# Two thirds of x loaded ahead of w1, w1's taps copied to contiguous places, small constants loaded later, and four turn copies moved to VectorE, in a dilated-attention and bottleneck kernel

## The chip, the cores and the metric

One core of one Trainium2 chip. The metric is the device time of one execution in microseconds (us), median of three runs. The work is fp32 throughout. An fp32 matmul runs as two passes over the array, so the profile's instruction counts on TensorE (PE) are twice the kernel's matmuls.

## The reference, cut to what matters

`x` is (4, 256, 64, 64). Layer 0 makes 49 attention weights for every pixel from a 7x7 convolution with dilation 2 and a 1x1 convolution, and then sums the 49 dilated shifts of `x` with them. Layer 1 is a bottleneck with batch norms that take their statistics from the data.

```python
# layer 0: w1 is (128, 256, 7, 7), w2 is (49, 128, 1, 1)
k = conv(x, w1, padding=6, dilation=2) + b1
k = conv(k, w2) + b2                                  # 49 logits a pixel
attn = softmax(k, axis=1)
xp = jnp.pad(x, ((0, 0), (0, 0), (6, 6), (6, 6)))
shifts = stack([xp[:, :, 2*u : 2*u+64, 2*v : 2*v+64] for u in range(7) for v in range(7)], axis=1)
x = einsum('bkchw,bkhw->bchw', shifts, attn)
# layer 1
h = relu(bn(conv(x, w1_1x1)))                         # 256 -> 64 channels
h = relu(bn(conv(h, w2_3x3, pad=1)))                  # 64 -> 64
h = bn(conv(h, w3_1x1))                               # 64 -> 256
out = relu(h + x)
```

## The kernel before, in words

**The convolution.** The two convolutions of layer 0 are one 7x7 convolution from 256 channels to 49, with the kernel w2·w1. Along the rows (the tap index u) the kernel uses a Winograd-like transform with the points ±0.4, ±0.8, ±1.25, ±2.5 (`PAIRS`), 0 and infinity. There are five **passes** over the data, one for each pair of points and one for the last two. In each, VectorE makes transformed rows of x (`xi`) out of sorted rows of x (`slots`) with `scalar_tensor_tensor` steps, all of which have the line L152, and PE multiplies them with the transformed weights `ut`, column tap by column tap (`column_convs`, L263). Columns come in four strips; `acc[i][s]` is the PSUM bank of strip s and of point i of the pair. [...]a first half of channels (up to about 293 us) runs all five passes, and each pass's sums are put aside in DRAM (`put_aside`, L287 and L288). The second half takes them back (`put_back`, L607, and ScalarE's copy from `bks` into PSUM, L608), adds its own and writes the logits (`outputs`: ScalarE's copy of one bank, L591, then VectorE's sum and difference, L592 and L593, and four steps of L152).

**The start of the first half.** x comes in three pieces of 16, 24 and 24 rows (`PIECES`), each with a load for each of four images: 12 loads in all, 0.62 or 0.93 MB each, on SP's DMA queue, into four rotating `raw` buffers. `sort_x` reads a piece and writes its rows to `slots` by four copies: rows by their remainder of 4, with the columns ahead of the rows, so that every element that a copy reads is apart from the next. Three of the four copies run on ScalarE (L171) and the last on POOL. `early(n, strips, parts)` makes those transformed rows of pass 0 that piece n completes, on VectorE; `even` and `odd` are three steps each and `mix` two.

The transformed weights need w1: half of it is two loads of 1.6 MB each (`load_w1`), into one buffer `w1raw`, so the second half's load waits until the first half's last reader is done. `product(w1raw, half, v, bank)` makes the weights of column tap v: seven matmuls (one for each u, L326), whose stationary operand is `w1raw[:, :, u * K7 + v]`, 128 elements that lie 49 elements apart; the moving operand `powers` are the w2 taps times the powers of the points. ScalarE evicts the result in two copies (L337, L338), and VectorE makes difference and sum of them (L342, L343). There are seven products for each half of the channels. The first `column_convs` need all seven products and the sums of pass 0.

**Around 293 us** the first half's passes end, `column_convs` of the second half's pass 0 start, and small constants are loaded on ScalarE's queue: the identity `ident`, `w1m`, `pavg`, `pdiff`, `w3m` and (L502 to L504) ten loads of batch-norm parameters into `bn12` and `bn3`. The tiles `bn12` and `bn3` are in the pool `keep`, which is open from the kernel's start; the other constants are in the pool `late`, which opens at L488 in memory that the first half's buffers leave.

In pass 2, every visit of a strip or of two strips has an `apply_factor` ahead of it, a VectorE step over two groups of 17 rows (17 = NR - 2; "17-wide" in the text).

**The end of layer 0.** For each of four strips VectorE and ScalarE make the softmax (`exponents`: VectorE's maximum and difference, ScalarE's exponential; `shares`: VectorE's sums and products, into padded rows `pads`). `turn(s, h)` transposes half a strip on PE (eight transposes, L567, in each of four steps j) into two of the eight PSUM banks, used in turn. Two copies for each step (g = 0 and 1) put the result into `amat` in `arena`. They are ScalarE's (L574), but with `shared=True` the g = 1 copies are VectorE's (L572). From 503 us on, PE sums the shifts with these weights (`gather`, L746), and conv1, conv2 and conv3 follow with their batch norms.

**What sets the order.** The engines' instruction orders are partly written by hand: within `manual_schedule(engines=...)` the named engines run in the order of the program. From the start to the end of layer 0's first half this holds for VectorE and PE, and for ScalarE and SP too in the block of L366 to L392. Where an engine isn't named, a scheduler places its instructions. Each engine runs its queue in order: an instruction that waits holds all behind it. The turns' order around the change is

```python
turn(1, 0); exponents(3); shares(2); turn(1, 1); turn(2, 0); shares(3)
load_xt(xtiles[1], *units[0], 1)
turn(2, 1, True); turn(3, 0, True); turn(3, 1, True)
```

Of the kernel before, what the change touches and what calls it, by code (L numbers as in the profile page):

```python
# [48 lines left out]
P = 128  # L49
B, C, H, W = 4, 256, 64, 64  # L50
NH = C // P
K7 = 7
# [41 lines left out]
def conv_seq_kernel(ctx: ExitStack, tc: tile.TileContext, xp, xt, w1, b1, w2t, b2, m1t, g1, be1,  # L94
# [6 lines left out]


    keep = pool(ctx, "keep", 1)
    bn12 = keep.tile([P, 4], F32, name="bn12")
    bn3 = keep.tile([P, 2, NH], F32, name="bn3")
    st1 = keep.tile([P, 2 * NT, 6], F32, name="st1")


# [49 lines left out]

    zero_rows(slots)

    def sort_x(raw, b, r0, n, dst, w0, last=None):

        d = dst.rearrange("p k (w b e) i -> p k w b e i", b=B, e=Q)
        nw = d.shape[2]
        for k in range(2):
            m = r0 // 2 + (r0 // 2 + 3 + k) % 2
            count = ((r0 + n) // 2 - m + 1) // 2
            i = (m + 3) // 2
            for a in range(2):
                lo = 2 * m + a - r0  # L170
                (last if last and k + a == 2 else nc.scalar.copy)(  # L171
                    d[:, k, :, PLACE[b], 2 * a : 2 * a + 2, i : i + count],
                    raw[:, lo : lo + 4 * count - 3 : 4, PAD + 2 * w0 : PAD + 2 * w0 + 2 * nw].rearrange(
                        "p r (w c) -> p w c r", c=2
                    ),
                )
# [60 lines left out]
    def strip(s, n=1):  # L237
        return slice(SW * s, SW * (s + n))
# [37 lines left out]
    with ExitStack() as s1:  # L276
# [13 lines left out]
        with ExitStack() as s2:  # L290
            w1p = pool(s2, "w1p", 1)
            rawp = pool(s2, "rawp", 4)
            b1row = w1p.tile([P, P], F32, name="b1row")
            b2sb = w1p.tile([1, K], F32, name="b2sb")
            ones = w1p.tile([1, P], F32, name="ones")
            nc.scalar.dma_start(out=w2sb, in_=w2t)
            nc.scalar.dma_start(out=b1sb, in_=b1[:, None])
            nc.scalar.dma_start(out=b2sb, in_=b2[None, :])
            nc.gpsimd.memset(ones, 1.0)


            powers = w1p.tile([P, K7, (1 + NP) * K], F32, name="powers")
            points = w1p.tile([P, NP], F32, name="points")
            for i, p in enumerate(PAIRS):
                nc.gpsimd.memset(points[:, i : i + 1], p)
            pv = powers.rearrange("p u (i k) -> p u i k", k=K)
            nc.vector.tensor_copy(pv[:, 0], w2sb.unsqueeze(1).to_broadcast([P, 1 + NP, K]))
            for u in range(1, K7):
                prev = pv[:, 0, 1:] if u == 1 else pv[:, u - 1, :NP]
                nc.vector.tensor_tensor(pv[:, u, :NP], prev, points.unsqueeze(2).to_broadcast([P, NP, K]), ALU.mult)  # L310
            nc.vector.tensor_copy(pv[:, K7 - 1, NP], w2sb)

            def load_w1(half):
                t = w1p.tile([P, P, K], F32, tag="w1", name="w1raw")
                for q in range(2):
                    c0 = half * P + 64 * q
                    nc.sync.dma_start(out=t[:, 64 * q : 64 * q + 64, :], in_=w1[:, c0 : c0 + 64, :])
                return t

            def product(w1raw, half, v, pw):  # L320

                for u in range(K7):

                    o = 0 if u == 0 else (2 + NP) * K if u % 2 else K
                    n = (1 + NP) * K if u in (0, K7 - 1) else NP * K
                    nc.tensor.matmul(  # L326
                        pw[:, o : o + n],
                        w1raw[:, :, u * K7 + v],
                        powers[:, u, :n],
                        start=(u == 0),  # L330
                        stop=(u == K7 - 1),
                        skip_group_check=True,
                    )
                c = slice((6 - v) * K, (7 - v) * K)
                ue = ut[:, half, 1 : 1 + NP, c]
                uo = pw[:, (2 + NP) * K : (2 + 2 * NP) * K].rearrange("p (i k) -> p i k", k=K)
                nc.scalar.copy(ue, pw[:, K : (1 + NP) * K].rearrange("p (i k) -> p i k", k=K))  # L337
                nc.scalar.copy(  # L338
                    ut[:, half, :: 1 + 2 * NP, c],
                    pw[:, : 2 * (1 + NP) * K].rearrange("p (a k) -> p a k", a=2)[:, :, :K],  # L340
                )
                nc.vector.tensor_tensor(ut[:, half, 1 + NP : 1 + 2 * NP, c], ue, uo, ALU.subtract)  # L342
                nc.vector.tensor_tensor(ue, ue, uo, ALU.add)  # L343

            def piece(n, b):
                r0, k = PIECES[n]
                raw = rawp.tile([P, 24, WP], F32, tag="raw", name="raw")
                nc.sync.dma_start(out=raw[:, :k], in_=xp[b, :P, r0 : r0 + k, :])
                sort_x(raw, b, r0, k, slots, 0, nc.gpsimd.tensor_copy)

            def early(n, cols=slice(None), parts=(even, odd, mix)):

                p, _, left = passes[0]
                t0, t1 = READY[n]
                x0, x1 = (xi[:, i, cols, t0:t1] for i in range(2))
                row = rows_of(slots, cols, READY[n])
                if even in parts:
                    even(p, left, row, x0)
                if odd in parts:
                    odd(p, left, row, x1)  # L360
                if mix in parts:
                    mix(p, x0, x1)

            bank = [acc[i][s] for s in range(NS) for i in range(2)]
            spare = [acc[i][s] for s in (NS - 1, 0) for i in range(2)]
            with tc.manual_schedule(engines={mybir.EngineType.Activation, mybir.EngineType.SP}):  # L366
                for b in range(B):
                    piece(0, b)
                w1a = load_w1(0)
                early(0)  # L370
                nc.scalar.copy(b1row, b1sb.to_broadcast([P, P]))
                nc.tensor.matmul(bank[7][:, :K], b1row, w2sb, start=True, stop=False)
                nc.tensor.matmul(bank[7][:, :K], ones, b2sb, start=False, stop=True)
                nc.scalar.copy(bias, bank[7][:, :K])
                for b in range(2):
                    piece(1, b)
                    product(w1a, 0, b, bank[b])
                for b in range(2, B):
                    piece(1, b)
                early(1, strip(0, 2), (even,))  # L380
                for v in range(2, 5):
                    if v > 2:
                        piece(2, v - 3)
                    product(w1a, 0, v, bank[v])
                early(1, strip(0, 2), (odd, mix))
                piece(2, 2)
                product(w1a, 0, 5, bank[5])
                piece(2, 3)
                early(2, strip(0), (even, odd))
                product(w1a, 0, 6, bank[6])  # L390
                early(2, strip(0), (mix,))
                w1b = load_w1(1)  # L392
            early(2, strip(1))
            early(1, strip(2, 2))
            for s in range(2, NS):
                early(2, strip(s))
            u = weights(0, 0)
            column_convs(0, u, True)
            column_convs(1, u, True)
            put_aside(0, 1)  # L400
            product(w1b, 1, 0, spare[0])
            apply_factor(slots, squares[0], NR - 1, strip(0, 2))
            for v in range(1, 5):
                product(w1b, 1, v, spare[v % 4])
            apply_factor(slots, squares[0], NR - 1, strip(2, 2), (0,))
            for v in range(5, K7):
                product(w1b, 1, v, spare[v % 4])
            apply_factor(slots, squares[0], NR - 1, strip(2, 2), (1,))
# [82 lines left out]
    w3m = late.tile([P, C], F32, name="w3m")  # L491
    pavg_sb = late.tile([P, P], F32, name="pavg_sb")
    pdiff_sb = late.tile([P, P], F32, name="pdiff_sb")
    nc.scalar.dma_start(out=ident, in_=z)
    nc.scalar.dma_start(out=w1m, in_=m1t)
    nc.scalar.dma_start(out=pavg_sb, in_=pavg)
# [59 lines left out]
    def turn(s, h, shared=False):  # L556

        row = pads[(2 * s + h) % 3]
        for j in range(4):
# [8 lines left out]
            for g in range(2):  # L568
                dst = amat[:, g, 2 * (2 * s + h) + j % 2, j // 2].rearrange("p (k n) e -> p k n e", k=2)
                src = pt[:, :, 64 * g : 64 * g + 64].rearrange("p (k w) n -> p k n w", k=2)  # L570
                if shared and g:
                    nc.vector.tensor_copy(dst, src)  # L572
                else:
                    nc.scalar.copy(dst, src)  # L574
# [556 lines left out]
```

## Time and profile before

| | us |
|---|---|
| Three runs | 813.88, 808.98, 813.5 (median 813.5) |
| The profiled execution | 815.58 |
| its span on the engines | 813.4 |

Busy time of three engines by stage in the profiled execution, in us:

| Stage, us from the span's start | PE | VectorE | ScalarE |
|---|---|---|---|
| 0 to 20: x pieces sorted, first `early` | 1.3 | 8.8 | 8.2 |
| 20 to 44.6: seven products | 23.5 | 11.3 | 17.8 |
| 44.6 to 56: rest of pass 0's sums | 0 | 11.0 | 4.3 |
| 56 to 100: column convolutions, second half's products | 42.6 | 41.9 | 4.4 |
| 100 to 122 | 19.0 | 19.5 | 13.7 |
| 122 to 309: passes of the first half | 186.6 | 161.1 | 52.7 |
| 309 to 463: passes of the second half | 148.0 | 146.1 | 22.8 |
| 463 to 505: softmax and turns | 40.1 | 28.6 | 30.6 |
| 505 to 813: gather, bottleneck | 280.8 | 145.5 | 146.1 |

The page's slices of the span show the same: a slice is 20.3 us, a digit is the busy share in tenths.

```profile
## 2 busy tenths in 40 slices
PE   0949989999999999979999999999999979979993
...
DVE  4489989999466999999999866122232337764695
ACT  4640165102541102111111268333444436344497
```

PE is at nine tenths nearly everywhere; the first three slices (to 61 us) are the widest hole, and the third (41 to 61 us) is at four tenths. ScalarE and VectorE reach four to six tenths in these three slices, and neither of them is full as an average over 20 us: whether one of them is what PE waits for is read from single waits.

The loads of that stage, from the page's DMA issues (size of each and median time from issue to landing):

```profile
raw<-in_xp_dram SPq DMA_DIRECT2D x36, 608.0 KB, 5.5
```

### The profile page before, as it was taken

Reading aid. Unit: us, or ns where it says so; the run is one execution under the profiler, and the core shown is the slowest. Engines: PE = TensorE matmul, PEld = TensorE weight load, DVE = VectorE, ACT = ScalarE, POOL = GpSimd, SP = SyncE. Lnnn points to the kernel's source line nnn. Section 1 sums busy time; section 2 is a strip of 40 time slices with the busy share of each in tenths; the row PEclk is TensorE's granted clock in tenths of the full one; section 3 lists DMA queues with packets and bytes.
Section 4 is the critical chain, followed back from the end, with each engine's and each line's share of the span. In section 5 each row is a group of like instructions: output and inputs, shape, how many; then the busy total and the mean of one; then the engine's idle time right before and its main releaser. Section 6 shows DMA issues by size and latency. Waiting matters only on the chain. (4 is left out here: it accounts for less than half of the span.)

```text
span 813.4 us, 10844 instructions
## 1 busy us (share of the span) xinstructions
PE 741.9 (91%) x4192; PEld 604.4 (74%) x4192; DVE 573.7 (71%) x673; ACT 300.4 (37%) x587; POOL 79.3 (10%) x137
## 2 busy tenths in 40 slices
PE   0949989999999999979999999999999979979993
PEld 0938968888888888858888889887888864439641
DVE  4489989999466999999999866122232337764695
ACT  4640165102541102111111268333444436344497
POOL 3210000001000010000003002222322200000000
PEclk9979998999999999998999999999999999998997
DMA  8931099703798876111110013666766669360298
GB/s 287 363 158 40 3 330 317 328 36 157 256 331 332 326 292 236 49 40 31 49 40 1 3 56 100 207 207 207 230 225 207 207 220 350 129 205 3 104 373 350
DMA packets 58949, 150.26 MB, mean 185 GB/s; under 512 B 7314, under 2 KB 35602, under 8 KB 54546
## 3 DMA queue, kind: packets, MB, share of 16 engines
q1 hardware_dynamic: 48624, 124.34, 43.4%
q10 hardware_dynamic: 10274, 25.23, 8.0%
q8 instruction: 33, 0.54, 0.3%
q14 instruction: 18, 0.15, 0.1%
HBM read 93.81 MB, written 55.74 MB: 184 GB/s over the span
## 5 line engine op out<-in xcount | busy, mean ns | idle before, releaser
L263 PE MATMUL acc<-arena 128*128 128x343 f32 (+3 forms) x2000 | 383.9, 355 | 20.8 <-DVE arena L152 20.6
L263 PEld LDWEIGHTS acc<-arena 128*128 128x128 f32 x2000 | 323.8, 193 | 79.9 <-issue 14.1
L152 DVE SCALAR_TENSOR_TENSOR arena<-arena 128x1024 f32<-128x1024 f32 (+7 forms) x192 | 290.6, 1560 | 28.0 <-PE acc L263 17.3
L746 PEld LDWEIGHTS acc<-arena,outer 128*128 128x128 f32 x1152 | 129.5, 192 | 8.5 <-issue 6.5
L746 PE MATMUL acc<-arena,outer 128*128 128x128 f32 (+1 forms) x1152 | 130.8, 275 | 1.8 <-POOL outer L126 1.8
L788 DVE BATCH_NORM_STATS2 st<-acc 128x6 f32<-128x512 f32 x16 | 11.1, 695 | 73.8 <-PE acc L780 73.7
L287 ACT COPY sv<-acc 128x392 f32<-128x392 f32 x40 | 19.0, 484 | 103.9 <-PE acc L263 101.7
L171 ACT COPY stage<-raw 128x128 f32<-128x128 f32 x128 | 43.7, 417 | 21.9 <-DMA raw<-in_xp_dram 21.5
L326 PE MATMUL acc<-powers,w1raw 128*128 128x196 f32 (+1 forms) x196 | 45.7, 397 | 6.3 <-DMA w1raw<-in_w_dram 4.9
L326 PEld LDWEIGHTS acc<-powers,w1raw 128*128 128x128 f32 x196 | 44.8, 315 | 6.9 <-issue 6.7
L591 ACT COPY outer<-acc 128x784 f32<-128x784 f32 x8 | 6.5, 812 | 101.1 <-PE acc L263 81.2
L124 ACT COPY outer<-outer 64x2304 f32<-64x2304 f32 x15 | 31.7, 2110 | 32.2 <-DMA outer<-in_xt_dram 27.7
L1007 PE MATMUL pconv<-arena,w3m 64*128 64x512 f32 x128 | 41.2, 635 | 0.0
L152 DVE SCALAR_TENSOR_TENSOR outer<-outer 128x784 f32<-128x784 f32 (+2 forms) x47 | 36.9, 839 | 3.6 <-DMA arena<-y_dram 3.6
L768 DVE COPY bks<-acc 128x256 f32<-128x256 f32 x32 | 12.1, 420 | 35.6 <-PE acc L746 35.6
L1007 PEld LDWEIGHTS pconv<-arena,w3m 64*128 64x128 f32 x128 | 19.1, 185 | 20.5 <-DVE arena L1065 15.4
L1069 ACT ACTIVATE outer<-arena 128x512 f32<-128x512 f32 x50 | 32.8, 749 | 3.7 <-DVE arena L844 1.4
L608 ACT COPY acc<-bks 128x392 f32<-128x392 f32 x40 | 18.5, 488 | 42.5 <-DVE outer L593 33.6
L1065 DVE SCALAR_TENSOR_TENSOR arena<-pconv,arena 128x512 f32<-128x512 f32 x50 | 33.3, 744 | 0.0
L125 POOL COPY outer<-outer 64x2048 f32<-64x2048 f32 x15 | 28.3, 1885 | 44.4 <-DMA outer<-in_xt_dram 43.6
L574 ACT COPY arena<-acc 128x512 f32<-128x512 f32 x52 | 27.1, 715 | 14.8 <-PE acc L567 14.4
L959 PE MATMUL pconv<-outer,arena 128*128 128x512 f32 x72 | 31.1, 592 | 0.0
(144 smaller groups left out, 627.4 us busy)
## 6 DMA issues: line engine op xcount, KB each, us to landing
raw<-in_xp_dram SPq DMA_DIRECT2D x36, 608.0 KB, 5.5
out_dram<-outer ACTq DMA_DIRECT2D x16, 1024.0 KB, 4.1
outer<-in_xt_dram SPq DMA_DIRECT2D x17, 896.0 KB, 5.8
arena<-y_dram SPq DMA_DIRECT2D x25, 512.0 KB, 8.6
fsort_dram<-stage SPq DMA_DIRECT2D x2, 4864.0 KB, 15.1
arena<-fsort_dram SPq DMA_DIRECT2D x8, 1216.0 KB, 10.6
y_dram<-outer SPq DMA_DIRECT2D x16, 512.0 KB, 4.7
aside_dram<-sv ACTq DMA_DIRECT2D x40, 196.0 KB, 5.8
```

Source lines behind the costliest of these rows:

```text
L124: nc.scalar.copy(t[:MID], x[MID:])
L125: nc.gpsimd.tensor_copy(t[MID:, :NT], x[:MID, 1:])
L152: nc.vector.scalar_tensor_tensor(out, in0, scalar, in1, ALU.mult, ALU.add)
L171: (last if last and k + a == 2 else nc.scalar.copy)(d[:, k, :, PLACE[b], 2 * a : 2 * a + 2, i : i + count], raw[:, lo : lo + 4 * count - 3 ...
L263: nc.tensor.matmul(acc[i][d][:, o : o + (hi - lo) * K], xi[:, i, CW * w : CW * w + CW, :].rearrange("p x t -> p (x t)"), u[i][:, lo * K : ...
L326: nc.tensor.matmul(pw[:, o : o + n], w1raw[:, :, u * K7 + v], powers[:, u, :n], start=(u == 0), stop=(u == K7 - 1), skip_group_check=True,)
L574: nc.scalar.copy(dst, src)
L746: nc.tensor.matmul(pt[:, o : o + hi - lo], x[:, i, half * P : (half + 1) * P], a[:, :, blocks, :].rearrange("p x m e -> p m x e"), start=( ...
L959: nc.tensor.matmul(m[k], wu[:, k, j, :], vs[k][:, g, j : j + R, :], start=(j == 0), stop=(j == 1))
L1007: nc.tensor.matmul(pt, w3m[part, half * P : (half + 1) * P], h2[part, slot, q, 512 * i : 512 * (i + 1)], start=True, stop=True)
L1065: nc.vector.scalar_tensor_tensor(v, conv3(b, q, i, half), sc3[:, half : half + 1], v, ALU.mult, ALU.add)
L1069: nc.scalar.activation(dst, v.rearrange("p (r w) -> p r w", w=R), AF.Relu, bias=sh3[:, half : half + 1])
```

## The change

The text of the change moves five things.

**1. Order of loads.** Pieces 0 and 1 of all four images are loaded and sorted ahead of `w1`. Piece 2 is loaded behind it. `bn12` and `bn3` leave the pool `keep` for `late`, so that the ten loads of L502 to L504 can't start before that pool opens.

```diff
     keep = pool(ctx, "keep", 1)
-    bn12 = keep.tile([P, 4], F32, name="bn12")
-    bn3 = keep.tile([P, 2, NH], F32, name="bn3")
...
     pdiff_sb = late.tile([P, P], F32, name="pdiff_sb")
+    bn12 = late.tile([P, 4], F32, name="bn12")
+    bn3 = late.tile([P, 2, NH], F32, name="bn3")
```

**2. Taps.** For the first half of the channels, ScalarE copies the seven taps u of one v (128 partitions x 896 elements) to a contiguous place in a free part of `arena`, three places in rotation; the matmuls read that. The second half's products still read `w1raw`.

```diff
+            def taps(w1raw, v):
+
+                o = UT + (2 + 2 * NP) * KV + K7 * P * (v % 3)
+                t = arena[:, o : o + K7 * P].rearrange("p (u c) -> p u c", c=P)
+                nc.scalar.copy(t, w1raw[:, :, v::K7].rearrange("p c u -> p u c"))
+                return t
+
+            wvs = {}
+
             def product(w1raw, half, v, pw):
 
+                wv = w1raw[:, :, v::K7].rearrange("p c u -> p u c") if half else wvs.pop(v)
                 for u in range(K7):
...
-                        w1raw[:, :, u * K7 + v],
+                        wv[:, u, :],
```

**3. Sorts.** Of piece 1, one copy in four (k + a == 0) goes to VectorE: four copies of 384 elements. Piece 2 is sorted in two halves of columns (192 elements a copy), the first for strips 0 and 1, and the second for strips 2 and 3, outside the block in which ScalarE's order is by hand.

```diff
-            def piece(n, b):
+            def load_piece(n, b):
                 r0, k = PIECES[n]
                 raw = rawp.tile([P, 24, WP], F32, tag="raw", name="raw")
                 nc.sync.dma_start(out=raw[:, :k], in_=xp[b, :P, r0 : r0 + k, :])
-                sort_x(raw, b, r0, k, slots, 0, nc.gpsimd.tensor_copy)
+                return raw
+
+            def sort_piece(raw, n, b, cols=0, strips=NS):
+                r0, k = PIECES[n]
+                on_dve = nc.vector.tensor_copy if n == 1 else None
+                sort_x(raw, b, r0, k, slots[:, :, strip(cols, strips)], WS * cols, nc.gpsimd.tensor_copy, on_dve)
```

**4. The order of the start,** which also sets VectorE's order of `early` sums among the products:

```diff
                 for b in range(B):
-                    piece(0, b)
+                    sort_piece(load_piece(0, b), 0, b)
+                early(0)
+                for b in range(B):
+                    sort_piece(load_piece(1, b), 1, b)
                 w1a = load_w1(0)
-                early(0)
...
-                for b in range(2):
-                    piece(1, b)
-                    product(w1a, 0, b, bank[b])
-                for b in range(2, B):
-                    piece(1, b)
-                early(1, strip(0, 2), (even,))
-                for v in range(2, 5):
-                    if v > 2:
-                        piece(2, v - 3)
+                early(1, strip(0, 2))
+                raws = []
+                wvs[0] = taps(w1a, 0)
+                for v in range(K7):
+                    if v + 1 < K7:
+                        wvs[v + 1] = taps(w1a, v + 1)
                     product(w1a, 0, v, bank[v])
-                early(1, strip(0, 2), (odd, mix))
-                piece(2, 2)
-                product(w1a, 0, 5, bank[5])
-                piece(2, 3)
-                early(2, strip(0), (even, odd))
-                product(w1a, 0, 6, bank[6])
-                early(2, strip(0), (mix,))
+                    if v < B:
+                        raws.append(load_piece(2, v))
+                        sort_piece(raws[v], 2, v, 0, 2)
+                    if v == 0:
+                        early(1, strip(2, 2), (even,))
+                    if v == 4:
+                        early(2, strip(0), (even, odd))
+                    if v == 5:
+                        early(2, strip(0), (mix,))
                 w1b = load_w1(1)
             early(2, strip(1))
-            early(1, strip(2, 2))
+            early(1, strip(2, 2), (odd, mix))
+            for b in range(B):
+                sort_piece(raws[b], 2, b, 2, 2)
             for s in range(2, NS):
                 early(2, strip(s))
```

**5. Turns.** In turn(1,1) and turn(2,0), the g = 1 copies of the odd steps j, four in all, go from ScalarE to VectorE. Both turns stand ahead of `shares(3)` in VectorE's order.

```diff
-                if shared and g:
+                if g and (shared or (j % 2 and (s, h) in ((1, 1), (2, 0)))):
                     nc.vector.tensor_copy(dst, src)
```

The orders of the engines that aren't by hand move with it: around 293 us, VectorE has three `visit` steps and one step of `apply_factor` ahead of the first L592 that stood behind it before, and one 17-wide step less after the fourth output group.

More of the change, by code (lines that the diff above doesn't have):

```diff
@@ L159, in conv_seq_kernel, with sort_x @@
     zero_rows(slots)
-    def sort_x(raw, b, r0, n, dst, w0, last=None):
+    def sort_x(raw, b, r0, n, dst, w0, last=None, first=None):
         d = dst.rearrange("p k (w b e) i -> p k w b e i", b=B, e=Q)
@@ L170, in sort_x @@
                 lo = 2 * m + a - r0
-                (last if last and k + a == 2 else nc.scalar.copy)(
+                (last if last and k + a == 2 else first if first and k + a == 0 else nc.scalar.copy)(
                     d[:, k, :, PLACE[b], 2 * a : 2 * a + 2, i : i + count],
```

## The prediction

> **What bounds the kernel now.** I read the page first: TensorE (PE) is busy 91% of the span, so the question is which PE gaps the change touches. The list of PE's waits, whole run (total us, times, longest), then three stretches of the timeline (start, us, engine, line, operation; in brackets the idle time before it and what ended it). "x98" counts two passes per fp32 matmul, so 49 matmuls.
>
> ```profile
> PE acc L263 <- DVE arena L152: 20.6, 3, 11.5
> ...
> PE acc L567 <- ACT arena L574: 1.8, 2, 1.4
> ```
> The start:
> ```profile
> 0.73 7.15 SPq L348 DMA_DIRECT2D raw<-in_xp_dram  x4
> ...
> 21.03 23.54 PE L326 MATMUL acc<-powers,w1raw 128*128 128x245 f32 x98 [4.95 <-DMA w1raw<-in_w_dram]
> ...
> 56.08 19.13 PE L263 MATMUL acc<-arena 128*128 128x196 f32 x86 [11.51 <-DVE arena L152]
> ```
> PE waits for w1 until 21.0, multiplies the seven products back to back until 44.6, then idles 11.5 us for VectorE's `early` sums. Around 300 us, where the small constants are loaded:
> ```profile
> 292.88 0.34 ACTq L494 DMA_DIRECT2D ident<-in_z_dram  x1
> ...
> 296.00 0.81 ACT L591 COPY outer<-acc 128x784 f32<-128x784 f32 x1 [19.87 <-DVE arena L152]
> ...
> 308.22 0.99 ACT L608 COPY acc<-bks 128x392 f32<-128x392 f32 x2 [5.92 <-DMA bks<-aside_dram]
> ...
> 308.76 36.65 PE L263 MATMUL acc<-arena 128*128 128x49 f32 x204 [0.24 <-ACT acc L608]
> ```
> PE is held 0.24 us by ScalarE's put-back copies: they are just in time, with no slack. The turns:
> ```profile
> 495.51 3.19 DVE L572 COPY arena<-acc 128x512 f32<-128x512 f32 x5 [2.90 <-ACT arena L574]
> 496.26 7.21 PE L567 MATMUL acc<-ident,outer 128*128 128x128 f32 x64
> ```
> VectorE had 2.9 us to spare there; PE did not.
>
> Two prices, by shape (busy, mean ns):
> ```profile
> L171 ACT COPY arena<-raw 128x384 f32<-128x384 f32 x24 | 19.1, 867 | 12.1 <-DMA raw<-in_xp_dram 7.0 <-DVE arena L152 5.1
> ...
> L171 ACT COPY arena<-raw 128x256 f32<-128x256 f32 x12 | 6.5, 630 | 0.1
> ```
> Back to back they step 0.79 and 0.58 us, so a half-column sort of 192 elements steps about 0.46.
>
> [...]sorts,[...] cost (867-630)/128 = 1.85 ns an element; the contiguous 2304-element copy at L124 takes 2110 ns, 0.92 an element. [...]granted clock 0.50 from 122.2 to 128.0, after a 3.1 us gap. [...]here 402 to 419 GB/s between 21 and 36 us.
>
> **Part 1, the start.** Removed: eight small issues of ScalarE's queue before its sorts, with the waits for `bn` and `b1` landings that held SP's first loads to 7.15 us. Moved: four loads of piece 1 (0.93 MB each) go ahead of w1 on SP's queue. Up to w1's landing 2.49+3.74+3.21 = 9.44 MB must pass: 23.0 us at 0.41 MB/us from about 2.9 us, plus 0.8 for the bubble before piece 1 (its buffers wait for the sorts, first freed near 8 us) and 0.8 to the landing: 27.5 instead of 21.0. VectorE in exchange gets `early(1)` of strips 0 and 1 done by about 35 (`early(0)` 12.7 to 22.1, its four new sort copies at 0.85, POOL's price, to 25.5, then 9.7 us); it cost nothing on the path if cheaper.
>
> From 27.5 on ScalarE sets the pace, in this built order: seven `taps` copies of 896 elements, seven evictions (L337+L338, 0.6), and 20 half-column sorts before the fifth eviction, eight of them of the *second* half, which the scheduler slid in between. A `taps` copy (T) is not in the trace: [...] I take 1.35. The first product starts cold, 5.05 as before (21.03 to 26.1), and its eviction waits for it in ScalarE's queue, with all sorts behind. So: 27.5 + 1.35 + 5.05 + 5*0.6 + 20*0.46 + 4*1.35 = 51.5 for the fifth eviction. PE's contiguous weight loads (315 to 193 ns) save about 0.4 us a product, beside that work: nothing. Behind the fifth eviction VectorE has, in order, its pair of L342/L343 (0.72), six `early(2, strip 0)` at 0.74, a pair, two `mix`, a pair: 8.1. Column convolutions start at 59.6, not 56.1: **+3.5**. VectorE is then 3.9 us (three even sums) ahead of its old plan, so PE's 1.36 us wait for L343 at 92.4 goes. Net **+2.2** (T = 0.93: 0.0; T = 1.85: +4.7; w1 a microsecond either way: one). What is late next is unchanged: the 3.1 us gap at 119 hangs on PE's last product through ScalarE's L338 and shifts with it. w1b's load now waits for the seventh `taps` (about 53) and lands by 64, before its use at 80: covered.
>
> **Part 2, small loads later.** The ten `bn` loads now stand on ScalarE's queue among those of 292.9 to 296.0, ahead of the copy at L591. DMA semaphores are used in turn, so a later issue waits for an earlier landing; in the changed program the fourth `bn` issue waits for `w1m`, which landed 8.6 us after its issue at 293.3, at 301.9. Eight issues of 0.55 follow: L591 starts at 306.3, not 296.0. VectorE, which in the new order does three `visit` steps and one `apply_factor` (5.8 us) ahead of L592, comes at 304.6, waits until 307.1 and ends L593 at 310.2. SP's put-back load waits for one of these `bn` landings too: issue near 305, landing 308 to 311.6 (4 to 6.3 us; before 6.3). The last put-back copy ends near 311.2, and PE has nine matmuls (0.384 each) behind that gate where it had six behind 308.8: 314.7 against 311.1, +3.6 (from +1 to +5). At 365 VectorE has one 17-wide step (2.35 us) less before the sums PE waits for: -2.35. Net **+1.25** (-1.4 to +2.7).
>
> **Part 3, four turn copies to VectorE.** They take 4*0.5 us off ScalarE, whose exponentials to 487.1, not these copies, set PE's 1.35 us wait at 488.2: no gain. On VectorE they stand ahead of `shares(3)`, and the last waits for PE's transposes of turn(2,0), 492.2, and ScalarE's copy after them: it ends at 493.65. `shares(3)` (2*2.45 us, begun at 486.45 before) ends at 498.5, and turn(2,1)'s VectorE copies, whose banks PE needs for turn(3,0), start then, not at 495.5. PE's 496.26 becomes 499.2: **+2.9** (0 if the copies overtook, +4 with the `xt` load that waits for `shares(3)`, SP's, 490.7 to 497.6).
>
> **Sum.** 2.2+1.25+2.9 = +6.3. Against the profiled execution's 815.6 (813.4 span and 2.2 around it) that is 821.9; it stands 2.1 above the median 813.5, so I say 820. `bn12`/`bn3` in another pool and the late sorts' 4 ScalarE and 4 POOL pieces (VectorE has 4.8 us of other steps before it needs them) cost nothing; without that cover 2 us.
>
> **Rivals.**
> 1. *Products at PE's pace.* If `taps` and sorts hide, products step 2.7 us (14 loads of 193 ns): 27.5+0.93+5.05+4*2.7+0.6 = 44.9, plus 8.1 = 53.0. Net of the 1.36: -4.4. With the 17-wide step off the path (-2.35) and turns at no cost: -6.8, so 807. For it: contiguous reads, an idle VectorE. Against it: ScalarE's 17.6 us list has no hole.
> 2. *ScalarE's queue becomes the bound* (slower). T at the sorts' rate (+4.7), part 2 at its upper end (+2.7), turns +2.9: +10.3, so 824. It passes 1% from T = 1.6 on with part 2 at its upper end (3.4+2.7+2.9 = 9.0). For it: the measured sort rate and the 8.6 us landing.
> 3. *It doesn't do what it says*: the moved pieces only trade waits, 812 to 816.
>
> **Chances.** Forecast 45%, rival 1 20%, rival 2 30%, rival 3 5%. Within 1% (8.1 us) is about what a measurement of this kernel can tell from no change. Forecast's cases beyond +8.1 (a third) and nearly all of rival 2 give slower 0.40; over half of rival 1, with the clock gap at 122 perhaps closing too (half clock for 5.8 us costs 2.9), gives faster 0.13; the rest 0.47. Range 806 to 828: rival 1's end less a microsecond, rival 2's with turns at +4 and w1 late by one and a half.
>
> **What would show it.** w1 landing near 27.5; a `taps` mean between 0.93 and 1.85 us; products with holes between them and first L263 near 59.6; L591 near 306 plus the shift; PE's first wait for L608 grown from 0.24 to some microseconds; turn(3,0) three microseconds later against turn(2,1). It is wrong if L263 starts before 56, or the small loads land within 3 us.

## The result, and the profile after

| | Before | Changed |
|---|---|---|
| Median of four runs, us | 813.07 | 820.64 |
| Lowest to highest | 808.98 to 813.88 | 818.87 to 821.26 |
| The profiled execution (its span) | 815.58 (813.4) | 820.12 (818.3) |

The ratio is 1.011 [1.0075, 1.0145]: the change made the kernel slower by about 1.1% (by the medians 7.6 us, 0.9%). In the changed kernel's line numbers, L334 is the product's matmul, L322 the `taps` copy, L345 and L346 ScalarE's evictions, L350 and L351 VectorE's, L150 VectorE's sums, L169 the sorts, L261 the column convolutions, L520 to L522 the `bn` loads, L609 and L626 what were L591 and L608, L585 the turns' transposes, L590 and L592 their copies.

PE's waits in the changed kernel (us in total, times, longest). In the kernel before, PE waited 4.9 us for w1's landing, 20.6 for VectorE's sums in three waits of L263, and 0.2 for L608:

```profile
PE acc L334 <- ACT arena L322: 10.0, 5, 4.5
...
PE acc L261 <- DVE arena L150: 3.8, 1, 3.8
...
PE acc L261 <- DVE arena L351: 3.5, 1, 3.5
PE acc L585 <- DVE arena L590: 3.4, 1, 3.4
PE acc L261 <- ACT sv L285: 3.0, 1, 3.0
PE acc L261 <- ACT acc L626: 2.7, 2, 2.3
```

VectorE's sums of pass 0 no longer hold PE as they did: the 11.5 us wait is gone. (In the third slice of the page before, 41 to 61 us, VectorE stands at eight tenths, not at four to six.) What came in its place is 10.0 us that end with a `taps` copy, 3.5 us behind the last product, and two waits: 2.7 for the put-back copies (0.2 before) and 3.4 for VectorE's turn copies (none before). Of the 10.0 us, 2.6 pass before w1 has landed (PE is idle from 26.6, w1 is there at 29.2), so some 7.4 are the copies' own. The starts of the same PE instructions in the two profiled executions show where it adds up:

| PE instruction | Before, us | Changed, us | Difference |
|---|---|---|---|
| First column convolutions | 56.08 | 61.54 | +5.46 |
| Second half's products | 76.77 | 80.36 | +3.59 |
| Column convolutions after them | 100.14 | 102.50 | +2.36 |
| After the gap near 122 | 122.15 | 124.42 | +2.27 |
| After the gap near 365 | 365.25 | 368.26 | +3.01 |
| turn(2,0) | 492.10 | 495.21 | +3.11 |
| turn(3,0) | 496.26 | 502.30 | +6.04 |
| Gathers | 503.30 | 511.00 | +7.70 |
| conv1 after the POOL wait near 563 | 565.28 | 570.83 | +5.55 |
| End of the span | 813.4 | 818.3 | +4.9 |

The start, from the timeline of the changed kernel (start, us, engine, line, operation, idle time before and its releaser):

```profile
29.21 3.49 ACT L322 COPY arena<-w1raw 128x896 f32<-128x896 f32 x2 [2.35 <-DMA w1raw<-in_w_dram]
31.07 7.57 PE L334 MATMUL acc<-powers,arena 128*128 128x245 f32 x28 [4.45 <-ACT arena L322]
...
47.86 2.76 PE L334 MATMUL acc<-powers,arena 128*128 128x245 f32 x14 [1.80 <-ACT arena L322]
48.51 0.36 ACT L345 COPY arena<-acc 128x196 f32<-128x196 f32 x1
48.72 0.56 ACT L169 COPY arena<-raw 128x192 f32<-128x192 f32 x1
49.14 0.28 ACT L346 COPY arena<-acc 128x98 f32<-128x98 f32 x1
49.27 1.42 ACT L169 COPY arena<-raw 128x192 f32<-128x192 f32 x3
...
50.54 1.83 ACT L322 COPY arena<-w1raw 128x896 f32<-128x896 f32 x1
...
53.26 0.30 ACT L346 COPY arena<-acc 128x98 f32<-128x98 f32 x1
...
61.54 13.78 PE L261 MATMUL acc<-arena 128*128 128x196 f32 x71 [3.49 <-DVE arena L351]
```

ScalarE runs without a hole from eviction to sort to sort to `taps`, and PE multiplies for 2.76 us and then waits 1.80 for the next copy. The fifth eviction ends at 53.6, and VectorE's list behind it takes the 8 us to 61.5.

Around 300 us:

```profile
295.44 0.62 ACTq L520 DMA_DIRECT2D bn<-in_be_dram  x1
...
298.15 0.47 ACTq L520 DMA_DIRECT2D bn<-in_g_dram  x1
...
303.92 0.48 ACTq L522 DMA_DIRECT2D bn<-in_be_dram  x1
304.44 0.81 ACT L609 COPY outer<-acc 128x784 f32<-128x784 f32 x1 [27.81 <-DMA bn<-in_be_dram]
304.55 0.99 SPq L625 DMA_DIRECT2D bks<-aside_dram  x2
305.28 0.49 ACT L626 COPY acc<-bks 128x392 f32<-128x392 f32 x1
...
305.83 6.59 PE L261 MATMUL acc<-arena 128*128 128x196 f32 x24 [2.34 <-ACT acc L626]
...
312.74 5.62 PE L261 MATMUL acc<-arena 128*128 128x49 f32 x29 [0.32 <-ACT acc L626]
```

ScalarE's queue stands still from 296.1 to 298.15, ahead of the third of the ten `bn` issues. The issues end at 304.4, and only then do L609 and the put-back copy for which PE waits get their turn. The turns:

```profile
496.19 0.69 DVE L590 COPY arena<-acc 128x512 f32<-128x512 f32 x1 [0.78 <-ACT arena L592]
496.80 0.96 DVE L553 TENSOR_REDUCE sm<-outer 128x16 f32<-128x784 f32 x1
...
501.56 3.18 DVE L590 COPY arena<-acc 128x512 f32<-128x512 f32 x5
...
502.30 8.87 PE L585 MATMUL acc<-ident,outer 128*128 128x128 f32 x64 [3.43 <-DVE arena L590]
```

The fourth moved copy ends at 496.9, `shares(3)` runs from there to 501.6, and the VectorE copies that free PE's banks come behind it. The 64 transposes then take 8.87 us; before they took 7.21.

### The profile page after: what moved, and what is told of

The parts are those of the page before. It is cut to its first block, busy times and chain, and to the rows that moved or that the text cites. A ratio compares the mean times of both kernels' runs of the same rounds, so it can differ in the third digit from the quotient of the medians.

```text
span 818.3 us, 10873 instructions
## 1 busy us (share of the span) xinstructions
PE 738.5 (90%) x4192; PEld 599.5 (73%) x4192; DVE 580.5 (71%) x681; ACT 308.3 (38%) x598; POOL 85.2 (10%) x141
## 5 line engine op out<-in xcount | busy, mean ns | idle before, releaser
L261 PE MATMUL acc<-arena 128*128 128x343 f32 (+4 forms) x2000 | 382.7, 354 | 12.9 <-DVE arena L150 3.8
L261 PEld LDWEIGHTS acc<-arena 128*128 128x128 f32 x2000 | 322.9, 192 | 71.7 <-issue 5.1
L150 DVE SCALAR_TENSOR_TENSOR arena<-arena 128x1024 f32<-128x1024 f32 (+7 forms) x192 | 291.5, 1560 | 23.1 <-PE acc L261 16.9
L169 ACT COPY stage<-raw 128x128 f32<-128x128 f32 x128 | 43.5, 416 | 22.5 <-DMA raw<-in_xp_dram 21.9
L609 ACT COPY outer<-acc 128x784 f32<-128x784 f32 x8 | 6.5, 813 | 101.5 <-PE acc L261 73.7
L150 DVE SCALAR_TENSOR_TENSOR outer<-outer 128x784 f32<-128x784 f32 (+2 forms) x47 | 36.8, 835 | 3.6 <-ACT outer L919 3.6
L626 ACT COPY acc<-bks 128x392 f32<-128x392 f32 x40 | 18.5, 487 | 42.2 <-DVE outer L611 30.1
L592 ACT COPY arena<-acc 128x512 f32<-128x512 f32 x48 | 25.6, 654 | 20.9 <-PE acc L585 20.8
L169 ACT COPY arena<-raw 128x192 f32<-128x192 f32 (+2 forms) x44 | 24.3, 627 | 16.4 <-DVE arena L150 16.4
L334 PE MATMUL acc<-powers,arena 128*128 128x196 f32 (+1 forms) x98 | 21.4, 376 | 10.1 <-ACT arena L322 10.0
```

What stands on the lines that cost most here:

```text
L150: nc.vector.scalar_tensor_tensor(out, in0, scalar, in1, ALU.mult, ALU.add)
L169: (last if last and k + a == 2 else first if first and k + a == 0 else nc.scalar.copy)(d[:, k, :, PLACE[b], 2 * a : 2 * a + 2, i : i + count],
L261: nc.tensor.matmul(acc[i][d][:, o : o + (hi - lo) * K], xi[:, i, CW * w : CW * w + CW, :].rearrange("p x t -> p (x t)"), u[i][:, lo * K : ...
```

## Experiments

Each was timed against the kernel before in five rounds. In the kernels named "before", the edit is made to the kernel before; the others start from the changed kernel. In the rounds of e1 to e10 the median of the kernel before was 811.1 to 811.9 us, so rows are compared by their ratios. The intervals of e1, e3, e4 and e9 overlap that of the whole change.

| Run | Median, us | Ratio to before, 95% interval |
|---|---|---|
| the change as a whole | 820.64 | 1.0110 [1.0075, 1.0145] |
| e1 no turn copies | 817.51 | 1.0070 [1.0052, 1.0089] |
| e2 no taps | 814.26 | 1.0034 [1.0020, 1.0047] |
| e3 taps read contiguously | 817.93 | 1.0081 [1.0065, 1.0097] |
| e4 small loads early | 818.91 | 1.0097 [1.0079, 1.0115] |
| e5 before, small loads late | 810.21 | 0.9995 [0.9973, 1.0017] |
| e6 before, small loads on SP | 808.90 | 0.9973 [0.9955, 0.9990] |
| e7 before, turn copies | 814.82 | 1.0042 [1.0026, 1.0058] |
| e8 three parts undone | 807.47 | 0.9946 [0.9925, 0.9966] |
| e9 taps on POOL | 820.38 | 1.0117 [1.0086, 1.0147] |
| e10 as e8, taps on POOL | 814.80 | 1.0045 [1.0026, 1.0064] |

### The turns: e1 and e7

```diff
-                if g and (shared or (j % 2 and (s, h) in ((1, 1), (2, 0)))):
+                if shared and g:
```

> The changed kernel with all copies of turn(1,1) and turn(2,0) back on ScalarE. Theory (the four copies delay shares(3), and PE then idles long enough to run at half clock): PE's 3.4 us wait ahead of turn(3,0) is gone, its 64 transposes take about 7.2 us instead of 8.9, the gathers start about 4.5 us earlier against turn(2,0); the 1.8 us wait for POOL's shift copy that the kernel before had in the gathers comes back, so the end moves by -2.4 to -2.7: about 818. Rival (the gathers absorb whatever the turns lose): within 0.5 of 820.6.

e7 makes the opposite edit in the kernel before.

> The kernel before with only the four turn copies on VectorE. Theory: PE waits 3.4 us ahead of turn(3,0) and then runs at half clock for some us, gathers start 4.5 later, 1.8 to 2.2 come back at the wait for POOL's shift copy near 565: +2.4 to +3.2. Rival (turns are hidden behind the gathers): within 0.5 of before.

PE's timeline in e1:

```profile
497.30 4.03 PE L585 MATMUL acc<-ident,arena 128*128 128x128 f32 x32
501.45 7.21 PE L585 MATMUL acc<-ident,outer 128*128 128x128 f32 x64
508.50 20.28 PE L764 MATMUL acc<-arena,outer 128*128 128x64 f32 x180
```

and in e7:

```profile
494.98 8.87 PE L567 MATMUL acc<-ident,outer 128*128 128x128 f32 x64 [3.45 <-DVE arena L572]
```

From turn(2,0) to the gathers e1 takes 11.2 us, the changed kernel 15.8. The wait and the slow transposes come and go with these four copies, in either kernel. The granted clock explains the second: from 504 to 506 us it is 0.50 in the changed kernel, and in e1 it is 1.00 in every 2 us from 490 to 512. Counted from turn(2,0), the end moves 4.0 us and not 4.6, since a part of a wait comes back: PE's wait for POOL's shift copy, 1.84 us near 563 in the kernel before, is gone in the changed kernel and is 0.6 in e1. By the ratios, the four copies cost 0.40% (3.2 us) here and 0.42% (3.4 us) there. The first of these is within the noise of its two intervals; that of e7, 1.0026 to 1.0058, leaves out 1. Hidden the copies are not.

### The taps: e2, e3, e9, e10

In e2 the products read `w1raw` in both halves.

```diff
-                wv = w1raw[:, :, v::K7].rearrange("p c u -> p u c") if half else wvs.pop(v)
+                wv = w1raw[:, :, v::K7].rearrange("p c u -> p u c")
...
-                wvs[0] = taps(w1a, 0)
...
-                    if v + 1 < K7:
-                        wvs[v + 1] = taps(w1a, v + 1)
```

> The changed kernel with the first half's products reading w1raw directly, no taps copies. Theory (ScalarE's queue, with seven copies of 1.79 us in it, sets the pace of the products): PE multiplies back to back from w1's landing at 29.2, 5.05 us for the first and 3.1 for each of six more, last product done near 53; column convolutions start near 56 instead of 61.5, total -4 to -5: about 816. Rival (contiguous weight loads are worth their copies, ScalarE isn't the pace): products step at 3.5 us or more, column convolutions no earlier than 60.5, total 820 to 822.

```profile
29.16 23.09 PE L334 MATMUL acc<-powers,w1raw 128*128 128x245 f32 x98 [2.71 <-DMA w1raw<-in_w_dram]
54.78 18.97 PE L261 MATMUL acc<-arena 128*128 128x196 f32 x100 [2.53 <-DVE arena L351]
```

PE multiplies without a gap from w1's landing, and the column convolutions start 6.8 us earlier than in the changed kernel. The ratio falls by 0.76%, about 6.2 us (4 to 5 were expected). This is the largest single part of the loss. PE's slower weight loads from strided places (315 ns on average, against 210 in the changed kernel) are in these 23.09 us and cost less than the copies.

In e3 each copy reads 896 elements in a row.

```diff
-                nc.scalar.copy(t, w1raw[:, :, v::K7].rearrange("p c u -> p u c"))
+                nc.scalar.copy(t, w1raw.rearrange("p c k -> p (c k)")[:, v * K7 * P : (v + 1) * K7 * P].rearrange("p (u c) -> p u c", c=P))
```

> The changed kernel with taps copies that read 896 contiguous elements of w1raw instead of 896 elements that lie 7 or 49 apart (so the weights are other elements of w1). Theory (the stride makes the copy 1.79 us): a copy takes about 0.93 us, ScalarE's list is 5 us shorter at the fifth eviction, column convolutions start near 56.5 instead of 61.5, total about -4: 816.5. Rival (the copy's time isn't its stride, or ScalarE isn't the pace): copies stay at 1.7 us or more, or they shorten and the column convolutions start within 1 us of 61.5, total 820 to 821.

From the groups by line in the start's stretch, first of the changed kernel, then of e3 (busy us, mean ns):

```profile
L322 ACT COPY arena<-w1raw 128x896 f32<-128x896 f32 x7 | 12.6, 1810 | 2.4 <-DMA w1raw<-in_w_dram 2.4
```
```profile
L322 ACT COPY arena<-w1raw 128x896 f32<-128x896 f32 x7 | 6.5, 947 | 0.0
```

The stride is the copy's price: 1810 ns against 947 for the same number of elements. The start was a miss, 59.55 instead of 56.5, although its first copies also read only w1's first part, and so begin 2.5 us earlier. The ratio's interval overlaps the whole change's: what e3 shows is the copy's price, not a gain. The timeline of e3 says what took the place:

```profile
38.80 0.52 ACT L169 COPY arena<-raw 128x192 f32<-128x192 f32 x1 [2.43 <-DVE arena L150]
...
42.01 7.93 PE L334 MATMUL acc<-powers,arena 128*128 128x245 f32 x28 [3.47 <-ACT arena L322]
```

A sort of piece 2 waits 2.43 us for VectorE's sums, which still read that part of `arena`; the next `taps` copy stands behind the sort in ScalarE's queue, PE idles 3.47 us for it, and its next two products run at a granted clock of 0.50 up to 47.5 us (they take 7.93 us instead of 5.6). Shorter copies don't help where the queue that they stand in waits for something else.

e9 leaves the copies as they are and moves them to POOL:

```diff
-                nc.scalar.copy(t, w1raw[:, :, v::K7].rearrange("p c u -> p u c"))
+                nc.gpsimd.tensor_copy(t, w1raw[:, :, v::K7].rearrange("p c u -> p u c"))
```

> The changed kernel with the taps copies on POOL, which is idle for most of that stage, instead of ScalarE. Theory (it is ScalarE's queue that held the products, not the copies as such): a copy takes about 1.7 us at the rate of POOL's sorts and hides behind a product of 2.75 us; products step at PE's pace, 30.9 + 5.05 + 6*2.75 = 52.5, column convolutions near 55, ratio to before about 1.003 as without taps. Rival (a copy ahead of each product costs PE wherever it runs, or POOL's copies are much slower): products step at 3.5 us or more, column convolutions at 58 or later, ratio 1.007 or more.

PE's part came as the theory has it: the last product ends at 52.65. But the start of the column convolutions and the ratio are the rival's, for a reason that neither theory named. VectorE's sums from 25 to 47 us, by shape, in the changed kernel and then in e9:

```profile
L150 DVE SCALAR_TENSOR_TENSOR arena<-arena 128x768 f32<-128x768 f32 x11 | 11.9, 1089 | 0.4
```
```profile
L150 DVE SCALAR_TENSOR_TENSOR arena<-arena 128x768 f32<-128x768 f32 x11 | 18.5, 1694 | 0.4
```

The same eleven sums take 6.6 us longer beside POOL's copies. What this costs goes through ScalarE, as in e3: a sort of piece 2 waits 4.15 us for these sums, and the evictions of the third to the fifth product stand behind it in ScalarE's queue. VectorE waits for each of them, so that it begins its list behind the fifth eviction at 52.7 us, 5.9 later than in e2 (46.8), and PE waits for the end of that list:

```profile
45.31 1.81 ACT L169 COPY arena<-raw 128x192 f32<-128x192 f32 x4 [4.15 <-DVE arena L150]
...
52.71 0.36 DVE L350 TENSOR_TENSOR arena<-arena,acc 128x196 f32<-128x196 f32 x1 [1.01 <-ACT arena L346]
...
60.60 5.83 PE L261 MATMUL acc<-arena 128*128 128x196 f32 x12 [7.94 <-DVE arena L351]
```

e10 repeats it without the other two losses:

> The version without the turn copies on VectorE and with the small loads on SP's queue, but with taps copied by POOL instead of left out. Theory: contiguous weight loads make a product 0.35 us shorter, 2.1 for six, less 1.7 for the first copy: within 1 us of the version without taps, ratio to before 0.994 to 0.997. Rival (POOL's copies hold PE): 0.998 or more.

The expectation was a miss: a sort waits 4.16 us for the sums here too, the column convolutions start at 61.00, after 8.0 us of waiting for VectorE, and the ratio is 1.0045 where the same version without taps has 0.9946.

### The small loads: e4, e5, e6

e4 puts the two tiles back into the pool `keep`.

> The changed kernel with bn12 and bn3 back in the pool that is open from the start, so the ten small loads are issued at the start again. Theory (late they cost PE 0.7 us net around 300 us, early they hold SP's first loads): piece 0 sorted 1.4 us later, w1 and the column convolutions about 1 us later, and -0.7 around 300: total 0 to +1, 820.6 to 821.6. Rival (the late small loads are the main loss): 817.5 to 818.5.

```profile
62.63 21.86 PE L263 MATMUL acc<-arena 128*128 128x196 f32 x100 [3.46 <-DVE arena L353]
...
367.63 97.66 PE L263 MATMUL acc<-arena 128*128 128x147 f32 x512 [5.99 <-DVE arena L152]
```

The start came as expected (column convolutions at 62.63, +1.1), and so did PE's waits: none for the put-back copies, and 5.99 ahead of 367.63 where the changed kernel has 3.76. The ratio, 1.0097, can't be told from the whole change's 1.0110: inside the changed kernel this part is worth about nothing, as its gain and its loss cancel. In the kernel before, the two sides can be seen apart. e5 makes the edit there:

> The kernel before with only bn12 and bn3 moved to the late pool. Theory (two sides of one edit): at the start SP's loads of piece 0 aren't held by small loads, and column convolutions start about 1.4 us earlier (54.7 instead of 56.1); around 300 us PE waits 2.3 to 3.7 us for the put-back copies (0.24 before), with half clock after it (1.3 to 2.6), and its wait at 365 shrinks by 2.2. Net -0.5 to +1.5 against before. Rival (late small loads are free): PE's wait for L608 stays under 0.5 us and the kernel is 1.4 or more faster than before.

```profile
54.03 21.22 PE L261 MATMUL acc<-arena 128*128 128x196 f32 x100 [11.47 <-DVE arena L150]
...
302.50 3.90 PE L261 MATMUL acc<-arena 128*128 128x196 f32 x16 [3.40 <-ACT acc L608]
307.68 52.79 PE L261 MATMUL acc<-arena 128*128 128x49 f32 x284 [1.28 <-ACT acc L608]
364.23 97.81 PE L261 MATMUL acc<-arena 128*128 128x147 f32 x512 [3.76 <-DVE arena L150]
```

The start gains 2.05 us (54.03 against 56.08); 4.4 more are waited around 300, and 2.2 less at 365. The sum is no measurable difference. e6 keeps the first and drops the second: the tiles stay in `keep`, and the ten loads are issued on SP's queue behind w1's second half, where SP has nothing to do until the first put-back.

```diff
                 w1b = load_w1(1)
+                for g in range(2):
+                    half = slice(g * MID, (g + 1) * MID)
+                    for i, a in enumerate((g1, be1, g2, be2)):
+                        nc.sync.dma_start(out=bn12[half, i : i + 1], in_=a[:, None])
+                nc.sync.dma_start(out=bn3[:, 0, :], in_=g3.rearrange("(n p) -> p n", p=P))
+                nc.sync.dma_start(out=bn3[:, 1, :], in_=be3.rearrange("(n p) -> p n", p=P))
...
-        for i, a in enumerate((g1, be1, g2, be2)):
-            nc.scalar.dma_start(out=bn12[half, i : i + 1], in_=a[:, None])
-    nc.scalar.dma_start(out=bn3[:, 0, :], in_=g3.rearrange("(n p) -> p n", p=P))
-    nc.scalar.dma_start(out=bn3[:, 1, :], in_=be3.rearrange("(n p) -> p n", p=P))
```

> The kernel before with the ten small loads issued on SP's queue behind w1's second half (bn12 and bn3 stay in the first pool). Theory: the start's gain of about 1.4 us without a cost at 300, where ScalarE's queue is as in before (PE's wait for L608 under 0.5 us): -1 to -2 against before. Rival (the start gains nothing because VectorE's sums wait for pieces that the DMA rate sets): column convolutions within 0.5 us of 56.1, total within 0.5 of before.

```profile
53.80 21.06 PE L263 MATMUL acc<-arena 128*128 128x196 f32 x100 [11.52 <-DVE arena L152]
```

Column convolutions start at 53.80, PE has no wait for the put-back copies, and the ratio is 0.9973 [0.9955, 0.9990].

### Three parts undone: e8

The changed kernel's order of loads and of VectorE's sums, with the edits of e1, e2 and e6 together.

> The changed kernel without taps copies, without the four turn copies on VectorE, and with the ten small loads on SP's queue behind w1's second half. Theory (the order of loads and of VectorE's sums is a gain, the three other parts are losses): column convolutions near 54.8, no wait at L626 near 306, no 3.4 us wait ahead of turn(3,0): -2 to -4 against before, faster than both. Rival (the parts' costs overlap, so undoing all brings no more than undoing the taps): 1.0034 of before as in that run, within 1 us.

```profile
28.91 23.51 PE L336 MATMUL acc<-powers,w1raw 128*128 128x245 f32 x98 [2.38 <-DMA w1raw<-in_w_dram]
54.97 18.98 PE L263 MATMUL acc<-arena 128*128 128x196 f32 x100 [2.55 <-DVE arena L353]
89.64 6.50 PE L336 MATMUL acc<-powers,w1raw 128*128 128x245 f32 x28 [0.19 <-DVE arena L353]
```

0.9946 is 4.4 us below before and 13 below the changed kernel. The first column convolutions start about a microsecond later than in e6, but PE's gap ahead of them is 2.55 us and not 11.5, PE keeps its clock behind it (the 100 passes take 18.98 instead of 21.06), and 1.16 us of waiting for L343 becomes 0.19. Half of the gain, 0.27 of 0.54%, e6 has without any of the new order. The other half fits loading two thirds of x ahead of w1, together with the new order of sums and the split sorts. These three were not separated, and the intervals of e6 and e8 overlap a little, so this half is likely and not shown.

From the changed kernel to e8 the ratio falls by 1.64%. The turns (e1) and the taps (e2) make 1.16 of it. The rest, about 0.5%, would be the small loads on SP's queue, if the parts add; that edit was not run alone on the changed kernel.

## Why the prediction was right, and where its terms were off

The forecast was slower by 6.3 us by three costs, 820 against a median of 813.5; the medians moved by 7.6, and 1.1% by the ratio is nearer 9. All three costs were there. That 820.64 lies so close to 820 is in part luck: part 1 was two microseconds too small, two terms that part 3 left out nearly cancel, and in the profile the clock gave back some three microseconds that no part of the sum had.

**Part 1** (+2.2 predicted). Two terms were too small. w1 landed at 29.2, not 27.5: the sum let the transfers run at 0.41 MB/us from 2.9 us on, but until 14 us the windows show 263 to 371 GB/s. The `taps` copy took 1.81 us, not the 1.35 that was taken, which was the author's estimate between two bounds. The upper bound, the sorts' rate, was right: 867 ns for 384 elements and 1.85 ns for each of 512 more make 1.81. The lower, 0.93, no trace showed before e3; its copies without the stride took 947 ns, so the stride is the reason. Together they make 3.5 us; the sorts (0.42 us each, not 0.46) and the evictions (2.2 us for five, not 3.0) gave 1.5 of it back. The first product took 5.1 us, as the sum has it: its passes step 0.33 us up to 35.3 us, those of the second product mostly 0.16. That this is a cold start is the author's reading; the record of the granted clock begins only at 35.8 us. So the fifth eviction ended at 53.6 instead of 51.5, and with VectorE's list of 8 us (8.1 predicted) the start lost 5.5 instead of 3.5. The wait of 1.36 us near 92 did vanish, as predicted. The profile comes to +2.4 only because the clock gave 1.9 back: the same 100 passes took 20.86 us before and 18.97 here. That is no merit of the change: after a gap of the same length (3.47 us) they took 21.86 in e1. The step failed in its size, and the profile hides it.

**Part 2** (+1.25 predicted; +0.7 in the profile between 124 and 368 us). ScalarE's queue did stop for a landing (as SP's did in the kernel before, where loads of x waited 5.5 us for `b1sb` to land and 5.2 for `bn`), but ahead of the third `bn` issue, which waits for `ident` (landed at 298.1), and not of the fourth. The fourth does wait for `w1m`, as the step says, but `w1m` had landed by 298.3, 5.8 us after its issue and not 8.6; why it was quicker stays open. The eight issues from the fourth on then took 5.7 us, not 4.4. So L609 ran at 304.4, which without the start's shift of 2.3 is 302.1, not 306.3. PE waited 2.7 us for the put-back copies (a delay of 3.6 predicted), and at another gate than the sum has it: 2.3 of them for the first copy, right behind L609, and 0.3 for the later one that waits for its load from DRAM. At the gap near 365 it waited 3.76 instead of 5.99 (the predicted -2.35 was -2.2). The half clock behind the new wait, 1.5 us, was not in the sum. The profile's +0.7 is smaller than these make it, because PE ran at half clock for 3.4 us behind the gap near 122, and for 6.0 before; half of that difference, about 1.3 us, is again no merit of the change. The start's side of this edit was not priced apart: e5 shows that it gains 2 us in the kernel before.

**Part 3** (+2.9 predicted; +2.9 measured at turn(3,0)). The chain was as written, to 0.1 us. Missing were two terms behind it: 1.7 us of half clock behind the new wait, and -2.2 us up to conv1, 1.84 of them PE's wait for POOL, which is gone.

**Rivals.** Products at PE's pace (807) needs the copies to hide; they stood on ScalarE's queue, which had no hole, and on an idle engine (e9) they slowed VectorE. Of the slower rival the copy's rate was right, but not the upper end around 300. That the parts only trade waits is true of the small loads alone.

## What to carry to other kernels

Ask of a copy that makes another engine faster what stands in the queue that it joins, and price a strided read by the nearest strided row, not by a contiguous one: here 12.6 us of copies bought PE some 0.5 to 0.6 us a product (back to back, products step 2.49 to 2.59 us in e9 and 3.09 in e2). Give small loads to a queue that is idle at that time, rather than to an earlier or later place on a busy one. A new PE wait of 2 to 4 us may bring half clock with it (1.5 to 2.9 us were lost behind such waits here, or nothing); a change that closes such a wait may win more than the wait.

## What the runs showed of the hardware that was not expected

**VectorE's sums and POOL's strided copies slowed each other.** A 768-element sum took 1.09 us in the changed kernel, where POOL had four short sorts in that stretch, and 1.69 in e9 beside POOL's strided copies; a POOL copy took 1.78 us where VectorE had no sums to do (at 45.6 us in e9) and 2.3 to 2.6 beside them. ScalarE's copies of the same data had no such effect (eight sums took 8.64 us beside them in the changed kernel, 8.59 without them in e2). Why the one pair of engines slowed and the other did not, the runs do not show.

**The clock after a gap depended on where the gap fell.** Ahead of the first column convolutions PE waited 3.46 to 3.49 us in four profiles of the same order of work (the changed kernel, e1, e3, e4). The 100 passes behind it took 18.97 and 18.98 us in two and 21.86 in the two others, with a granted clock of 0.50 for some 6 us there. The record of the granted clock in the traces shows what differs. In ten profiles (the kernel before, the changed kernel, e1 to e8; e5 to e8 up to 518 us), the stretches at 0.50 begin whole multiples of 3.41 us from one another, and all but a profile's last are one to four times 3.41 us long. In the changed kernel they begin at 124.60, 305.48, 366.92 and 503.48 us, 53, 71 and 111 times 3.413 us behind the first. So the clock changed on a grid of 3.41 us. In e1 and e4, 2.5 us of the gap lie in one interval of this grid, and the next interval runs at 0.50. In the changed kernel and e3 the grid cuts the gap into 1.7 and 1.8 us, and the clock stays.

So a shorter gap cost more than a longer one. Near 305 us the changed kernel waited 2.34 us, 2.0 of them in one interval, and the next 3.4 us ran at 0.50; near 300 us e2 waited 3.80 us, cut into 1.9 and 1.9, and kept its clock. The exact limit is not shown: 1.96 us kept the clock in e3 near 302, and 1.89 lost it in e5 near 361. No interval had to be idle throughout: 2.0 of its 3.41 us were enough near 305 us.

Where the grid lies differs from profile to profile: before the first column convolutions it has a line at 59.75 us in the changed kernel and at 57.75 in e3. A profile of one execution can therefore hide or add 3 us at such a gap (18.97 us against 21.86 for the same 100 passes): two profiles are compared gap by gap, not by their ends.
